# Attention scores and output rows on quarters of the TensorE array, and smaller background steps, in a fused two-layer kernel

## The chip, the cores and the metric

The kernel runs on one core of a Trainium2 chip. A core has TensorE (PE, matmul, with its weight loads shown as PEld), VectorE (DVE), ScalarE (ACT), GpSimd (POOL) and SyncE (SP), which issues transfers. They run side by side and wait for each other through semaphores. The metric is the device time of one execution in microseconds; the profile is of one such execution.

## The reference

Two layers on x of 2 x 512 x 32 x 32, all in 32-bit floats. The first is an attention with deformable keys, followed by an MLP:

```python
q = _gconv1x1(xn, qw)                         # 8 groups of 64 channels
off = tanh(pw @ gelu(depthwise 6x6, stride 4 of q)) * 4      # 8x8 key positions per group
kv = _grid_sample(xn, nx, ny)                 # 64 sampled keys per group
k = _gconv1x1(kv, kw); v = _gconv1x1(kv, vw)
bias = sign(pos) * log1p(abs(pos))            # pos: 1024 queries x 64 keys x 2, per group
bias = relu(bias @ cpb_w1 + cpb_b1)           # 128 wide
bias = relu(bias @ cpb_w2 + cpb_b2)           # 128 x 128
bias = bias @ cpb_w3 + cpb_b3
attn = softmax(qh @ kh^T * DH**-0.5 + bias)   # 16 groups (2 images x 8 heads)
x = x + out_w @ (attn @ v) + out_b
x = x + mlp(bn(x))                            # 512 -> 2048 -> 512
```

The second layer is a full self-attention over the 1024 positions of each image with 512 channels. The bias network is the largest part: for each of the 16 groups, 1024 x 64 pairs pass through a 128 x 128 layer.

## The kernel before, in words

**The loop.** 256 slices (`NS = NG * NSL`), 16 for each of the 16 groups; a slice holds four keys against all 1024 queries. In each slice VectorE makes the first layer (`st_layer1`, L616), TensorE multiplies by `cpb_w2` (`st_layer2`, L633): four PSUM tiles `ps2` of 128 x 1024, each made of two times four matmuls that use 32 columns of the array each. ScalarE empties them with a relu (L640 and L642), VectorE adds pairs (`st_sum`, L650), and transfers with addition join them further (`st_fold` L664, `st_join` L667 and L669, and L652). The pool `zp` has three PSUM tiles, shared by the slices' tiles and by all background work (`flat`); `simp` has two tiles of half that size, for the scores. Every fourth slice a table is loaded from DRAM (`load_tables`, L587, buffer `fb`, one deep) and turned into two by ScalarE (`st_tables`, L597 and L604). Every fourth slice, too, `st_layer3` adds the third layer's result of four slices into the score tile `sim` of the group (L698).

**Scores.** In the last `st_layer3` of each group four matmuls add queries times keys into `sim` (L682). The keys lie in `kz` with zeros in the half of the 128 rows that belongs to the other group, so all 128 rows of the array are used, with 32 columns a matmul.

**Background.** `later()` yields small steps, one per slice, issued behind the slice's last eviction (`tc.issue_after(evicted[s][1])`). It runs five chains (`CHAINS`), each for one or two pairs of groups. `chain` makes the queries (L265, copied by L270), the 36 taps of the depthwise convolution on ScalarE (L312; `TAPS` says how many taps go into a step, each once per pair), the offsets, and stores the logarithms for the tables to DRAM (L391, from the result of L389). `sample` weighs and samples the keys (L412 to L461), and multiplies them: keys by L468, output rows (values already multiplied by the output weights, `uo`) by L469, copied by L470 and L473. The sampled keys stand in `kvz`, zeroed by GpSimd (L451), with each group's in its own half of the columns.

**Softmax.** `softmax_steps` is a second generator, advanced once per slice: the scores leave PSUM (L712), are turned (L723, L725), then the maximum (L730, L731), exponentials (L736), reciprocals (L741), normalisation (L745), and the turning back into `qa` (L754, L757). For most pairs both groups go together (n = 2). One `tail` is active at a time.

**Start.** Ahead of the loop come the ranks (L206 to L222), which sort the 128 hidden channels by the sign of their weights for `arrange`; the first chain, step by step (`head`); and products of the second layer's weights (`weights`, L521). ScalarE's and SyncE's queues issue the input transfers in the order of the code; one that needs a semaphore already in use waits for the earlier transfer.

**After the loop** stand the output projection (L875), the MLP (L928) and the second layer (L1047, L1123, L1145).

A scheduler fixes each engine's order when the program is built; the code's order, the pools and `issue_after` decide it. The functions that the change touches, with their lines:

Of the kernel before, what the change touches and what calls it, by code (L numbers as in the profile page):

```python
# [8 lines left out]
F32 = mybir.dt.float32  # L9
# [10 lines left out]
J = 64  # L20
# [5 lines left out]
CHAINS = [[(0, 0)], [(0, 1)], [(0, 2), (0, 3)], [(1, 0), (1, 1)], [(1, 2), (1, 3)]]  # L26
HEAD = 3
TAPS = [36, 12, 6, 4, 4]
NU = 4
# [18 lines left out]
def conv_seq_kernel(ctx: ExitStack, tc: tile.TileContext, x, xt, kst, pst, cst, vec, wsm, outw, w1, w2, wl, out):  # L48
    nc = tc.nc


# [28 lines left out]

    kz = cp.tile([P, NCH * B, 2, J], F32, name="kz")

# [56 lines left out]
    with tc.tile_pool(name="lp", bufs=2) as lp:  # L139
# [27 lines left out]
        nc.scalar.dma_start(out=ws[:, 0:P], in_=wsm[:, 0:P])  # L167
        nc.scalar.dma_start(out=ws[:, 1024:1408], in_=wsm[:, 1536:1920])
        nc.scalar.dma_start(out=cs, in_=cst)

# [3 lines left out]
        )  # L174
        nc.scalar.dma_start(out=pz[:, 0:413], in_=pst)
        nc.scalar.dma_start(out=ident, in_=kst)

        def load(b, k):
# [26 lines left out]
        perm, place = pw_[:, 256:384], pw_[:, 384:512]  # L205
        nc.gpsimd.memset(one, 1.0)  # L206
        nc.gpsimd.tensor_scalar(po_, wb[:, 0:1], 0.0, None, ALU.is_ge)
        ps = flat("rank")
        nc.tensor.matmul(ps[:, 0:1], tri, po_, start=True, stop=True)
        nc.tensor.matmul(ps[:, 512:513], one, po_, start=True, stop=True)  # L210
        nc.scalar.copy(rn, ps.rearrange("p (h n) -> p h n", h=2)[:, :, 0])
        r_, n_ = rn[:, 0:1], rn[:, 1:2]
        nc.gpsimd.tensor_scalar(pc, chan, n_, r_, ALU.add, ALU.subtract)
        nc.gpsimd.tensor_scalar(dc, pc, r_, po_, ALU.subtract, ALU.mult)
        nc.gpsimd.tensor_tensor(pc, pc, dc, ALU.subtract)
        nc.vector.tensor_scalar(k16, four, n_, 4.0, ALU.is_le, ALU.mult)
        nc.vector.tensor_reduce(t4, k16, AX.X, ALU.add)
        free, bound = ([t.rearrange("p (a b l) -> p b a l", a=2, b=2)[:, i] for t in (place, crow)] for i in (0, 1))
        nc.vector.tensor_scalar(bound[0], bound[1], t4, 64.0, ALU.is_ge, ALU.mult)
        nc.vector.tensor_tensor(bound[0], bound[0], bound[1], ALU.add)  # L220
        nc.vector.tensor_scalar(free[0], free[1], t4, None, ALU.add)
        nc.vector.tensor_scalar(perm, place, pc, None, ALU.is_equal)  # L222

# [24 lines left out]
        def chain(ci):  # L248
# [3 lines left out]
            for i in range(K):  # L252
                k = k0 + i
                if i == 0:
                    xn = xn0 if ci == 0 else load(b, k)
                    yield
                nc.scalar.activation(xn, xn, AF.Identity, bias=col("bn1b", k), scale=bns[:, k : k + 1])
                if ci > 0:
                    yield
                ps = flat("psq")  # L260

                quads = [(slice(64 * f, 64 * f + 64), slice(64 * h, 64 * h + 64), f, h)
                         for f in range(2) for h in range(2)]
                for f_, h_, f, h in quads:
                    nc.tensor.matmul(  # L265
                        ps[h_, f * 512 : (f + 1) * 512], wq[f_, k * P + 64 * f : k * P + 64 * f + 64],
                        xn[f_, h * 512 : (h + 1) * 512], start=True, stop=True,
                    )
                for f_, h_, f, h in quads:
                    nc.scalar.copy(  # L270
                        qa[f_, b, k, h * 512 : (h + 1) * 512], ps[h_, f * 512 : (f + 1) * 512]
                    )
                if i + 1 < K:
                    xn = load(b, k + 1)
                yield
# [123 lines left out]
        def sample(ci):  # L399
# [23 lines left out]
            for i, (b, k) in enumerate(G):  # L423
# [20 lines left out]
                for t in range(8):  # L444
                    for f in range(2):
# [3 lines left out]
                        )  # L449
                kvz = ph.tile([P, 2, J], F32, name="kvz")  # L450
                nc.gpsimd.memset(kvz, 0.0)  # L451

                for f in range(2):
                    r = slice(64 * f, 64 * f + 64)
                    d = kvz[r, f, :].rearrange("p (e i t) -> p e i t", e=2, t=8)
                    v, u = (
# [8 lines left out]

                ps = flat("pkk")
                kf = kvz.rearrange("p f j -> p (f j)")
                nc.tensor.matmul(ps[:, 0:P], wk[:, k * P : (k + 1) * P], kf, start=True, stop=True)  # L468
                nc.tensor.matmul(ps[:, 512:1024], kf, uo[:, k, :], start=True, stop=True)  # L469
                nc.scalar.activation(  # L470
                    kz[:, g].rearrange("p f j -> p (f j)"), ps[:, 0:P], AF.Copy, scale=DH ** (-0.5)
                )
                nc.scalar.copy(vp[:, g, :], ps[:, 512:1024])  # L473
                yield
# [83 lines left out]
        head, g, n, v = chain(0), weights(0), weights(1), vectors()  # L558
        for _ in range(HEAD):
            next(head)  # L560
        next(g)
# [110 lines left out]
        def st_layer3(s):  # L672
            gi, i = divmod(s // 4, NSL // 4)
            b, k, f = groups[gi]
            if i == 0:
                sims[gi] = simp.tile([P, 512], F32, name="sim")
            if i == NSL // 4 - 1:
                assert state[chain_of[b, k][0]] is None
                for h in range(2):
                    for e in range(2):  # L680
                        q = 64 * h + 32 * e
                        nc.tensor.matmul(  # L682
                            sims[gi][q : q + 32, :], kz[:, b * NCH + k, f, 32 * e : 32 * e + 32],
                            qa[:, b, k, h * 512 : (h + 1) * 512], start=False, stop=False,
                        )
            w = w3f[:, 24 - 8 * i : 56 - 8 * i]
# [6 lines left out]
            for m in range(len(parts[1])):  # L693
                for h in range(2):
                    for e in range(2):
                        if m < len(parts[e]):
                            q, (w_, t) = 64 * h + 32 * e, parts[e][m]
                            nc.tensor.matmul(  # L698
                                sims[gi][q : q + 32, :], w_, t[:, h, :], start=(i == 0),
                                stop=(i == NSL // 4 - 1 and m == len(parts[e]) - 1),  # L700
# [5 lines left out]
        def softmax_steps(gi):  # L706
# [27 lines left out]
            for a in range(8):  # L734
                for i in range(n):
                    nc.scalar.activation(  # L736
                        e[:, a, i], e[:, a, i], AF.Exp, bias=mx[:, a, i : i + 1], accum_out=sm[:, a, i : i + 1]
                    )
                if a % 2 == 1:
                    yield  # L740
            nc.vector.reciprocal(sm[:, :, 0:n], sm[:, :, 0:n])  # L741
            yield
            for a in range(8):
                for i in range(n):
                    nc.scalar.activation(e[:, a, i], e[:, a, i], AF.Copy, scale=sm[:, a, i : i + 1])  # L745
                if a % 4 == 3:
                    yield
# [12 lines left out]

        tail = None
        bg = later()
# [4 lines left out]
        for s in range(NS):  # L767
# [31 lines left out]
            if bg is None and s > ready and (s - ready) % 4 == 0 and (s - ready) // 4 <= 8:  # L799
# [3 lines left out]
                else:  # L803
                    fold(nc.vector, op0[0], which=(i - 4,))
            if tail is not None:
                with tc.issue_after(evicted[s][s % 4 == 0]):
                    tail = tail if next(tail, 0) is None else None
            if s % 4 == 3 and s >= 7:
                st_layer3(s - 7)
                if (s - 3) % NSL == 0:  # L810
                    tail = softmax_steps(s // NSL - 1)
        st_sum(NS - 1, 2)
        st_layer3(NS - 4)
        tail = softmax_steps(NG - 1)
        next(tail)
# [515 lines left out]
```

## Time and profile before

| | |
|---|---|
| median of 3 runs | 2697.14 us (2695.79 to 2699.49) |
| profiled execution | 2695.95 us, span 2694.2 us |
| first to last tile of L633 | from 45.2 us to about 1945 us |
| passes of L633 | 16384, busy 1784.1 us |
| passes of L682 (queries times keys) | 128, busy 17.3 us |
| passes of L468 and L469 (keys, output rows) | 16 and 16, busy 3.9 and 8.2 us |
| ACT L312 / L736 / L745 | taps / exponentials / normalisations of the background |
| granted TensorE clock | 0.999 |

A row of the profile gives line, engine, operation, output<-input by the program's names, shapes, count, busy time and mean duration of one, then the engine's idle time before it and what ended it. A matmul of 32-bit floats appears as two passes, so 16384 passes are 8192 matmuls. Four matmuls on different columns or quarters of the array run together: their passes start a few ns apart. In the timeline the columns are start, length, engine and operation; SPq is SyncE's queue of transfers. The ends of matmuls are modelled.

### The profile page before, as it was taken

Reading aid. Unit: us, or ns where it says so; the run is one execution under the profiler, and the core shown is the slowest. Engines: PE = TensorE matmul, PEld = TensorE weight load, DVE = VectorE, ACT = ScalarE, POOL = GpSimd, SP = SyncE. Lnnn points to the kernel's source line nnn. Section 1 sums busy time; section 2 is a strip of 40 time slices with the busy share of each in tenths; the row PEclk is TensorE's granted clock in tenths of the full one; section 3 lists DMA queues with packets and bytes.
Section 4 is the critical chain, followed back from the end, with each engine's and each line's share of the span. In section 5 each row is a group of like instructions: output and inputs, shape, how many; then the busy total and the mean of one; then the engine's idle time right before and its main releaser. Section 6 shows DMA issues by size and latency. Waiting matters only on the chain.

```text
span 2694.2 us, 47017 instructions
## 1 busy us (share of the span) xinstructions
PE 2668.7 (99%) x19644; PEld 961.0 (36%) x19644; DVE 2239.4 (83%) x1337; ACT 1681.3 (62%) x2166; POOL 575.6 (21%) x625
## 2 busy tenths in 40 slices
PE   9999999999999999999999999999999999999999
PEld 3323323333432333233333333333344444446455
DVE  5999999998999899999999999999764484466354
ACT  4788797789878887877777786787622131114041
POOL 1222222222222222222222222222243223000000
PEclk9999999999999999999999999999999999999999
DMA  5667666766666766767677676776631110000000
GB/s 186 149 146 148 155 139 137 159 147 147 141 146 146 154 137 137 155 141 149 141 155 145 143 152 145 148 150 141 128 128 47 47 47 31 16 16 0 31 1 31
DMA packets 95219, 314.05 MB, mean 117 GB/s; under 512 B 17184, under 2 KB 19872, under 8 KB 92320
## 3 DMA queue, kind: packets, MB, share of 16 engines
q0 software_dynamic: 57168, 201.88, 40.2%
q1 hardware_dynamic: 36832, 108.02, 11.3%
q8 instruction: 155, 2.54, 0.4%
q10 hardware_dynamic: 1008, 1.15, 0.1%
q14 instruction: 56, 0.46, 0.0%
HBM read 71.67 MB, written 6.55 MB: 29 GB/s over the span
## 4 chain that ended last, share of the span: by engine, by line
PE 88%; ACT 4%; DMA 3%; issue 2%; DVE 2%; POOL 0%; ACTq 0%; DVEq 0%; POOLq 0%; SPq 0%
PE ps L633 57%; PE sw L928 14%; PE sw L1047 9%; PE sim L698 2%; PE sw L1145 2%; DMA ua<-ua 1%; DMA ua<-uo 1%; PE psg L521 1%; PE sw L875 1%; ACT prod L312 1%; ACT rx L640 1%; DVE h L616 1%; ACT ub L642 1%; PE sim L682 0%; ACT sx L745 0%
## 5 line engine op out<-in xcount | busy, mean ns | idle before, releaser
L633 PE MATMUL ps<-h,cw 128*32 128x512 f32 x16384 | 1784.1, 593 | 14.6 <-ACT rx L640 14.2
L616 DVE CUSTOM_DVE_ANT_1 h<-ta,tb 128x4096 f32<-128x4096 f32 (+1 forms) x257 | 1132.3, 4406 | 47.4 <-PE ps L633 43.1
L633 PEld LDWEIGHTS ps<-h,cw 128*32 128x32 f32 x16384 | 536.2, 110 | 1231.3 <-issue 1130.1
L640 ACT ACTIVATE rx<-ps,sc 128x1024 f32<-128x1024 f32 x512 | 568.7, 1111 | 203.2 <-PE ps L633 187.8
L642 ACT ACTIVATE ub<-ps,sc 128x1024 f32<-128x1024 f32 x256 | 307.9, 1203 | 89.8 <-PE ps L633 89.4
L650 DVE SCALAR_TENSOR_TENSOR ub<-rx,sc,ub 128x1024 f32<-128x1024 f32 x256 | 327.6, 1280 | 5.8 <-ACT ub L642 5.6
L652 POOL DMA_DIRECT2D ua<-ub x128 | 114.7, 896 | 726.9 <-DVE ub L650 698.8
L652 POOL DMA_DIRECT2D uo<-ub x127 | 117.6, 926 | 388.0 <-DVE ub L650 317.5
L928 PE MATMUL sw<-xb,w1t 128*128 128x512 f32 x448 | 193.7, 592 | 1.3 <-DVE xs L121 1.3
L928 PE MATMUL sw<-hm,w2t 128*128 128x512 f32 x448 | 193.6, 592 | 0.0
L642 ACT ACTIVATE ua<-ps,sc 128x1024 f32<-128x1024 f32 x128 | 154.0, 1203 | 57.1 <-PE ps L633 56.8
L642 ACT ACTIVATE uo<-ps,sc 128x1024 f32<-128x1024 f32 x128 | 153.9, 1202 | 40.1 <-PE ps L633 38.0
L650 DVE SCALAR_TENSOR_TENSOR ua<-rx,sc,ua 128x1024 f32<-128x1024 f32 x128 | 164.1, 1282 | 16.4 <-ACT ua L642 16.3
L669 POOL DMA_DIRECT2D ua<-uo x126 | 108.4, 861 | 321.2 <-DMA ua<-uo 306.1
L650 DVE SCALAR_TENSOR_TENSOR uo<-rx,sc,uo 128x1024 f32<-128x1024 f32 x128 | 164.1, 1282 | 11.8 <-ACT uo L642 11.7
L121 DVE TENSOR_TENSOR hm<-hm,sw 128x1024 f32<-128x1024 f32 x56 | 67.6, 1219 | 112.5 <-PE sw L928 112.3
L664 POOL DMA_DIRECT2D ua<-ua x126 | 152.7, 1212 | 5.3 <-DMA ua<-ub 4.2
L928 PEld LDWEIGHTS sw<-xb,w1t 128*128 128x128 f32 x448 | 85.0, 190 | 108.8 <-issue 104.8
L937 ACT ACTIVATE hm<-hm,vs 128x512 f32<-128x512 f32 x64 | 42.6, 713 | 129.5 <-DVE hm L121 129.5
L928 PEld LDWEIGHTS sw<-hm,w2t 128*128 128x128 f32 x448 | 85.1, 190 | 107.1 <-issue 106.2
L121 DVE TENSOR_TENSOR xs<-xs,sw 128x1024 f32<-128x1024 f32 (+1 forms) x48 | 55.5, 1171 | 74.6 <-PE sw L1047 36.0
L1047 PE MATMUL sw<-aT,vt 128*128 128x512 f32 x224 | 96.7, 593 | 0.3 <-ACT aT L1127 0.3
(238 smaller groups left out, 1797.8 us busy)
## 6 DMA issues: line engine op xcount, KB each, us to landing
ua<-ub POOLq DMA_DIRECT2D x128, 512.0 KB, 4.8
uo<-ub POOLq DMA_DIRECT2D x127, 512.0 KB, 5.0
fb<-fdr SPq DMA_DIRECT2D x64, 512.0 KB, 5.3
ua<-ua POOLq DMA_DIRECT2D x126, 256.0 KB, 6.3
ua<-uo SPq DMA_DIRECT2D x126, 256.0 KB, 2.4
ua<-uo POOLq DMA_DIRECT2D x126, 256.0 KB, 4.0
w1t<-in_w SPq DMA_DIRECT2D x8, 1024.0 KB, 4.9
w2t<-in_w SPq DMA_DIRECT2D x8, 1024.0 KB, 4.8
```

The source lines that it names most:

```text
L121: nc.vector.tensor_tensor(out, a, b_, op)
L616: nc.vector._custom_dve(TENSOR_ADD_SAT, out=h1[:, y : y + step].rearrange("p y t x -> p (y t x)"), in0=a.unsqueeze(1).to_broadcast([P, ste ...
L633: nc.tensor.matmul(ps[32 * q : 32 * q + 32, h, :], cw2[:, 32 * z : 32 * z + 32], h1[:, 16 * h : 16 * h + 16, q, :], start=True, stop=True,)
L640: nc.scalar.activation(o, ps, AF.Relu, bias=sc[:, 4 + z : 5 + z])
L642: nc.scalar.activation(o, ps, AF.Relu, bias=sc[:, 4 + z : 5 + z], scale=sc[:, z : z + 1])
L650: nc.vector.scalar_tensor_tensor(r[1], r[0], sc[:, z : z + 1], r[1], ALU.mult, ALU.add)
L652: nc.gpsimd.dma_start(out=sums[s][1], in_=sums[s][3], accum_op=ALU.add)
L664: nc.gpsimd.dma_start(out=lanes(s, 0), in_=lanes(s, 1), accum_op=ALU.add)
L669: nc.gpsimd.dma_start(out=lanes(s, 1), in_=lanes(s + 1, 0), accum_op=ALU.add)
L698: nc.tensor.matmul(sims[gi][q : q + 32, :], w_, t[:, h, :], start=(i == 0), stop=(i == NSL // 4 - 1 and m == len(parts[e]) - 1),)
L928: nc.tensor.matmul(ps[:, m, :], w[:, a, k, m * P : (m + 1) * P], x[:, b_, k, :], start=(k == 0), stop=(k == 1),)
L1047: nc.tensor.matmul(ps[:, m, :], w[:, a, k, c + m * P : c + (m + 1) * P], x[b_][:, k, :], start=(k == 0), stop=(k == nk - 1),)
```

## The change

Five edits:

1. `kz` holds each pair's keys without zeros, 64 columns. In the last `st_layer3` of the first group of a pair, four matmuls of 64 rows and 64 columns (`QUADS`) give queries times keys of both groups, and the second group's score tile is taken then.
2. In `sample` the keys stand in `kv` without zeros or memset; keys are one matmul of 64 columns, output rows four matmuls of 64 x 64 with 256 columns each, in a PSUM tile of their own, copied by four instructions.
3. `TAPS` goes from 6, 4, 4 to 4, 3, 3 for the last three chains.
4. With two groups together the softmax yields after every pair of exponentials and every fourth normalisation; waiting generators stand in the list `tails`, since one now takes more than 16 slices.
5. The ranks become `rank()`, called after the first chain's queries; two input transfers change places.

```diff
-TAPS = [36, 12, 6, 4, 4]
+TAPS = [36, 12, 4, 3, 3]
...
+    QUADS = [(slice(64 * f, 64 * f + 64), slice(64 * h, 64 * h + 64), f, h) for f in range(2) for h in range(2)]
...
-    kz = cp.tile([P, NCH * B, 2, J], F32, name="kz")
+    kz = cp.tile([P, NCH * B, J], F32, name="kz")
...
         nc.scalar.dma_start(out=ws[:, 0:P], in_=wsm[:, 0:P])
-        nc.scalar.dma_start(out=ws[:, 1024:1408], in_=wsm[:, 1536:1920])
-        nc.scalar.dma_start(out=cs, in_=cst)
...
         nc.scalar.dma_start(out=pz[:, 0:413], in_=pst)
+        nc.scalar.dma_start(out=ws[:, 1024:1408], in_=wsm[:, 1536:1920])
         nc.scalar.dma_start(out=ident, in_=kst)
+        nc.scalar.dma_start(out=cs, in_=cst)
...
+        def rank():
...
-                kvz = ph.tile([P, 2, J], F32, name="kvz")
-                nc.gpsimd.memset(kvz, 0.0)
+                kv = ph.tile([P, J], F32, name="kv")
...
-                ps = flat("pkk")
-                kf = kvz.rearrange("p f j -> p (f j)")
-                nc.tensor.matmul(ps[:, 0:P], wk[:, k * P : (k + 1) * P], kf, start=True, stop=True)
-                nc.tensor.matmul(ps[:, 512:1024], kf, uo[:, k, :], start=True, stop=True)
-                nc.scalar.activation(
-                    kz[:, g].rearrange("p f j -> p (f j)"), ps[:, 0:P], AF.Copy, scale=DH ** (-0.5)
-                )
-                nc.scalar.copy(vp[:, g, :], ps[:, 512:1024])
+                ps, pk = flat("pkv"), flat("pkk")
+                nc.tensor.matmul(pk[:, 0:J], wk[:, k * P : (k + 1) * P], kv, start=True, stop=True)
+                for f_, h_, f, h in QUADS:
+                    nc.tensor.matmul(
+                        ps[h_, f * 512 : f * 512 + 256], kv[f_, :], uo[f_, k, h * 256 : (h + 1) * 256],
+                        start=True, stop=True,
+                    )
+                nc.scalar.activation(kz[:, g], pk[:, 0:J], AF.Copy, scale=DH ** (-0.5))
+                for f_, h_, f, h in QUADS:
+                    nc.scalar.copy(vp[f_, g, h * 256 : (h + 1) * 256], ps[h_, f * 512 : f * 512 + 256])
...
-        for _ in range(HEAD):
-            next(head)
+        next(head)
+        next(head)
+        rank()
+        next(head)
...
-            if i == 0:
+            if gi not in sims:
                 sims[gi] = simp.tile([P, 512], F32, name="sim")
-            if i == NSL // 4 - 1:
+            if f == 0 and i == NSL // 4 - 1:
...
-                for h in range(2):
-                    for e in range(2):
-                        q = 64 * h + 32 * e
-                        nc.tensor.matmul(
-                            sims[gi][q : q + 32, :], kz[:, b * NCH + k, f, 32 * e : 32 * e + 32],
-                            qa[:, b, k, h * 512 : (h + 1) * 512], start=False, stop=False,
-                        )
+                sims[gi + 1] = simp.tile([P, 512], F32, name="sim")
+                for f_, h_, o, h in QUADS:
+                    nc.tensor.matmul(
+                        sims[gi + o][h_, :], kz[f_, b * NCH + k, :], qa[f_, b, k, h * 512 : (h + 1) * 512],
+                        start=(o == 1), stop=False,
+                    )
...
-                if a % 2 == 1:
+                if n == 2 or a % 2 == 1:
                     yield
...
-                if a % 4 == 3:
+                if a % (4 // n) == 4 // n - 1:
                     yield
...
-            if tail is not None:
+            if tails:
                 with tc.issue_after(evicted[s][s % 4 == 0]):
-                    tail = tail if next(tail, 0) is None else None
+                    if next(tails[0], 0) is not None:
+                        tails.pop(0)
...
-                    tail = softmax_steps(s // NSL - 1)
+                    tails.append(softmax_steps(s // NSL - 1))
```

## The prediction

> **What bounds the kernel now.** I read the busy times first, then the same by stage, then the waits of TensorE (PE), then the rows and the timeline of what the change touches.
>
> ```profile
> span 2694.2 us, 47017 instructions
> ...
> PE 2668.7 (99%) x19644; PEld 961.0 (36%) x19644; DVE 2239.4 (83%) x1337; ACT 1681.3 (62%) x2166; POOL 575.6 (21%) x625
> ...
> PE 88%; ACT 4%; DMA 3%; issue 2%; DVE 2%; POOL 0%; ACTq 0%; DVEq 0%; POOLq 0%; SPq 0%
> ```
>
> PE is busy nearly always and carries 88% of the chain that ended last. The rest of the chain shows where PE had to wait. By stage (columns: stretch, length, then busy time of PE, weight load, VectorE, ScalarE, GpSimd):
>
> ```profile
> 1000.00:1200.00 200.00, 197.62 (x1860) 61.16 (x1856) 197.45 (x115) 160.33 (x222) 47.69 (x55) 1.00 0.68 145
> 1200.00:1947.00 747.00, 747.00 (x6948) 228.73 (x6944) 706.59 (x329) 553.86 (x646) 181.43 (x206) 1.00 0.69 145
> ```
>
> From 1200 us on, when the chains are finished, PE never stops; all its idle time lies before. The main wait of PE between 45 and 1200 us (us in total, times, longest):
>
> ```profile
> PE ps L633 <- ACT rx L640: 14.2, 13, 2.7
> ```
>
> So in the loop PE waits for ScalarE (ACT) to empty PSUM, 13 times; two more waits are of 0.2 us. These gaps count only what lies beyond modelled ends. By the starts of consecutive passes (normally 0.43 us from group to group) I get 18.6 us in 17 places, a cold-clock stretch at 833 us included. ACT's timeline shows the cause at one of them:
>
> ```profile
> 151.22 1.21 ACT L642 ACTIVATE ub<-ps,sc 128x1024 f32<-128x1024 f32 x1 [0.60 <-PE ps L633]
> 152.32 3.59 ACT L312 ACTIVATE prod<-qa,vs 128x49 f32<-128x49 f32 x12
> 155.81 1.10 ACT L640 ACTIVATE rx<-ps,sc 128x1024 f32<-128x1024 f32 x1
> ```
>
> Twelve taps hold ACT 3.5 us between two evictions, and PE's next tile starts 0.82 us late (0.93 a slot later). So ACT may be away about 2.65 us before PE notices.
>
> **What the Trainium skill says.** "TensorEngine Tiling (Array Packing)", Tiling Modes, has four independent 64x64 tiles, and says that changing the tiling mode drains TensorE. The trace agrees: the L265 quads run together, and PE's steps into and out of them are longer (below). Its Performance Considerations warn that tiling doesn't speed up PSUM evacuation; the waits above are of that kind. "ScalarE: Activation LUTs", What ACT_TABLE_LOAD costs, gives 1283 ns a table load; here it takes 1.28 us.
>
> **The change, part by part.** PE first. Starts in PE's timeline and in the rows by form:
>
> ```profile
> 195.85 1.04 PE L682 MATMUL sim<-qa,kz 128*32 128x512 f32 x8
> 196.71 1.04 PE L698 MATMUL sim<-ua,w3f 128*32 128x512 f32 x8
> ...
> 604.35 1.09 PE L265 MATMUL psq<-xn,ws 64*64 64x512 f32 x8
> 605.37 3.64 PE L633 MATMUL ps<-h,cw 128*32 128x512 f32 x32
> ...
> 297.61 0.49 PE L468 MATMUL pkk<-kvz,ws 128*128 128x128 f32 x2
> 297.93 1.02 PE L469 MATMUL pkk<-vp,kvz 128*128 128x512 f32 x2
> 298.89 7.50 PE L633 MATMUL ps<-h,cw 128*32 128x512 f32 x68
> ```
>
> *Queries times keys.* Before, 16 groups of four 32-column matmuls, in the mode of their neighbours: 0.86 us each (195.85 to 196.71), 13.7 us. After, 8 groups of four 64x64 matmuls of the form of L265: 1.02 us (604.35 to 605.37), 0.11 more at the entry (0.52 from the last L633 pass to L265, against 0.41) and 0.02 behind: 1.16 us, 9.3 us. Gain 4.5 us, not the 6.9 us that halving would give; two mode changes take the rest.
>
> *Keys and output rows.* Before, 297.61 to 298.89 is 1.28 us, with entry and exit 1.42 us, 8 times. After: 64 columns instead of 128 in the first product (some 0.16 + 0.16 us, by the first steps of other small matmuls), then quads of 256 columns, half of L265's passes (0.25 us to the second pass, 0.31 us from it to L633), with one more mode change: about 1.01 us. Gain 0.4 x 8 = 3.2 us. PE's work so falls by **7.7 us**, in a stage where PE is the bound.
>
> *What this costs at PSUM.* The step now takes two of the three PSUM tiles instead of one. The next slice's first tile must then wait for the last tile of the slice before: its eviction starts 0.23 us after its end and takes 1.20 us (L642), 0.1 us to PE, so 1.5 us, while the new matmuls cover 1.0 us. 0.5 us of wait, 8 times: **+4.4 us** at 0.55 (from 0, if ACT is early, to 1.0 each where it is late). ACT itself gets four 64-partition copies of 256 (0.59 us at 512, L270; about 0.37) for one of 0.58: 0.9 us more a step, under the 2.65 us that it may be away. The memset of kvz leaves GpSimd, busy 21%: nothing.
>
> *Smaller steps.* No work is removed from ACT; pile-ups get smaller. I went through ACT's instruction order in the changed program slot by slot, with 0.29 us a 64-wide tap, 0.41 us a 128-wide, 0.33 us an exponential with its accumulator, 0.24 us a normalisation, and compared with 2.65 us:
> - chain 1 keeps its 12 taps: 1.7 us of wait stay.
> - chain 2 (slots 40 to 53): before 1.30 + 2.87 + 1.67 + 0.37 = 6.2 us. After, 8 taps with 2 exponentials or 4 normalisations, 3.3 to 3.8 us at three places, and an output transpose behind them: 0.8 + 1.1 + 0.6 + 1.1 = 3.6 us.
> - chains 3 and 4: 6 taps; 0.16 + 0.40 + 1.16 + 1.14 + 0.66 = 3.5 us become 0.6; the exponentials of slot 104 (2.69 + 1.41 us, behind a maximum that VectorE reached late) 0.7; the normalisations beside L431 and L434 (1.24 + 0.85) 0.5.
> - chain 4's gelu now falls between exponentials (slot 138), which reload their table: 2 x 1.28 us in one slot. 0.95 us become 2.4.
>
> Sum after: 1.7 + 4.4 + 3.6 + 0.6 + 0.7 + 0.5 + 2.4 = 13.9 against 18.6: **-4.7 us**.
>
> *What the finer steps make late.* Chain 2 ends three slots later, and its table is wanted in slot 60. In the trace of before:
>
> ```profile
> 473.06 0.42 DVE L389 SCALAR_TENSOR_TENSOR fe<-fe 64x256 f32<-64x256 f32 x1
> ...
> 474.62 1.41 ACT L597 ACTIVATE ta<-fb,vs 128x512 f32<-128x512 f32 x1
> ...
> 473.51 5.42 SPq L391 DMA_DIRECT2D fdr<-fe  x4
> 479.10 1.70 SPq L587 DMA_DIRECT2D fb<-fdr  x1
> ```
>
> Call E the end of L389 (473.5), in slot 56; ACT asks for a table at E + 1.1. After, the same instruction stands in slot 59, so slot 60 asks at E + 1.1 + 6.9 = E + 8. But SyncE issues four stores (to E + 5.5), then a join of two partial sums (0.5 us), then the load, which lands 5.3 us later (median of L587): E + 11.4. ACT is 3.4 us late, with the evictions of the slice behind it. Of this some 0.9 us is cover: the two table operations take 1.7 us (1.13 + 0.58 from start to start) of the 2.65 us that ACT may be away. **+2.6 us** once (0 to 6). Chains 3 and 4 end 20 slots before their tables are wanted.
>
> *Start.* PE idles at 6.9 to 9.0 us before the rank matmul, for pst (landed at 8.9); only then come the queries, whose input was ready at 7.5. The swap lets them go first, but cst now goes last (issued at about 5.4 us, landing at some 9.3 by the 3.7 us of the transfer whose place it takes), and GpSimd's hb (L188), which waits for it, stands ahead of the sign test that the ranks need: sign at 10.5, the weight products at 11.0 instead of 10.8. **+0.2 us** (-1.4 to +1.7): VectorE's convolution starts 1.9 us sooner and takes the rank's 1.4 us in, and the loop's start stays PE's (45.2).
>
> Sum: -7.7 - 4.7 + 2.6 + 0.2 = **-9.6 us**. The profiled execution took 2695.95 us, span 2694.2, the median 2697.14; the difference belongs to every run, so 2697.1 - 9.6 = **2687.5 us**.
>
> **Rivals.**
> *More:* the new waits are hidden (kv's 4.4, chain 2's 3.6, the table's 2.6, the small ones): -7.7 - 18.6 + 1.7 + 2.4 + 0.2 = -22, 2675 us. For it: PE starts later at each of them if any earlier wait has let ACT catch up. Against: the wait at kv follows from three tiles.
> *Given back:* kv waits 1.0 us each (+3.6 more) and the table 6 us (+3.4): -2.6, 2694.5 us, no difference to be told. For it: VectorE is busy 98% at 1000 to 1200 us, so late chains don't catch up.
> *Slower:* the quads don't run together. Queries times keys writes both groups' banks, the output rows read quarters of an operand. Serial, a group costs 4 x 0.86 + 0.3 = 3.7 instead of 1.16 (+2.5, 8 times: 20 us), the kv quads +1.3 x 8 = 10: 2717 us. It decides from 0.94 us more on each of the 16 groups. Against: L265 has the same rows, columns and two banks, and its eight passes start in two bunches of four, 6 ns apart.
> That the change does nothing is excluded: its program has 32 such matmuls instead of 64.
>
> **How the numbers follow.** 2687.5 has 0.62 (own range 2682 to 2692), more 0.14, given back 0.16, slower 0.08. About 0.2% (5.4 us) can be told from no change. Faster 0.76, same 0.16, slower 0.08. The range takes in "given back" and the better half of the distance to "more": 2679 to 2697.
>
> **What would show it.** Right: sim<-qa,kz with 64 passes instead of 128, about half of the busy time of L682 (17.3 us) plus mode changes; waits of PE for L640 and L642 in total some 4 to 5 us fewer, with new ones of 0.5 us at the kv steps; one wait of ACT's table (L597 before) for fb of some 3 us near 470 us; PE at 100% from 1200 us on. Wrong: passes of the new groups 0.43 us apart; no wait at the kv steps; a wait for fb over 6 us or none; the loop starting over 2 us from 45.2.

## The result, and the profile after

The changed kernel took 2690.70 us in the median (2687.49 to 2691.74), the kernel before, beside it on the same chip, 2698.18 us (2695.79 to 2699.49): a ratio of 0.9971, 95% interval 0.9954 to 0.9989, 7.5 us less (3.0 to 12.4 by the interval). The forecast was 9.6 us less. Part of that closeness is luck: 4.4 us of forecast waits did not come, while about 3 us in PE's passes and 2.1 us more for a late table came unforecast, and that table was late for another reason than the one given.

The page of the changed kernel, its first lines and its chain of work:

```profile
span 2688.9 us, 46981 instructions
...
PE 2664.8 (99%) x19628; PEld 955.2 (36%) x19628; DVE 2244.6 (83%) x1337; ACT 1689.0 (63%) x2191; POOL 575.3 (21%) x617
...
PE 85%; DVE 6%; issue 4%; ACT 2%; DMA 2%; SPq 0%; POOL 0%; DVEq 0%; POOLq 0%; ACTq 0%
```

PE is the bound as before. The same two stages (stretch, length, then busy time of PE, weight load, VectorE, ScalarE, GpSimd):

```profile
1000.00:1200.00 200.00, 196.51 (x1844) 60.41 (x1840) 199.07 (x115) 166.80 (x228) 48.09 (x54) 1.00 0.67 142
1200.00:1942.00 742.00, 742.00 (x6904) 227.79 (x6896) 703.01 (x332) 555.16 (x662) 179.71 (x204) 1.00 0.69 145
```

From 1200 us on PE never pauses, as before; all its pauses lie ahead of that. The waits of PE between 45 and 1200 us (us in total, times, longest):

```profile
PE ps L638 <- ACT rx L645: 10.7, 12, 3.0
PE ps L638 <- DVE kv L461: 1.4, 1, 1.4
```

The first is 14.2 us in 13 places in the kernel before. There are no new waits behind the steps that make keys and output rows, where eight of about 0.5 us were forecast. Their price is there, in another form. PE's timeline around one scores step and one step of keys and output rows (columns: start, length, engine, line, operation, output<-input, shape, passes):

```profile
197.49 1.09 PE L687 MATMUL sim<-qa,kz 64*64 64x512 f32 x8
198.51 1.06 PE L703 MATMUL sim<-ua,w3f 128*32 128x512 f32 x8
...
299.44 0.43 PE L468 MATMUL pkk<-kv,ws 128*128 128x64 f32 x2
299.80 0.66 PE L470 MATMUL pkv<-vp,kv 64*64 64x256 f32 x8
300.39 0.62 PE L703 MATMUL sim<-ua,w3f 128*32 128x512 f32 x1
300.84 0.62 PE L638 MATMUL ps<-h,cw 128*32 128x512 f32 x2
300.85 0.59 PE L703 MATMUL sim<-ua,w3f 128*32 128x512 f32 x1
300.85 14.32 PE L638 MATMUL ps<-h,cw 128*32 128x512 f32 x126
314.60 0.60 PE L703 MATMUL sim<-ua,w3f 128*32 128x512 f32 x3
```

The quads of queries times keys run together: 1.02 us from their first pass to the third layer. The last lines show what was not forecast. Directly behind the quads of 299.80 stands one single matmul of the third layer (L703), a quarter of a group of four; its three partners come at 314.60. Nothing fills the other three quarters of the array for 0.45 us. Six of the eight steps have such a lone quarter in the changed program's instruction list, against two groups that are split in the program before. By the rows per form of the kernel before, and then of the changed one:

```profile
L698 PE MATMUL sim<-ua,w3f 128*32 128x512 f32 x504 | 68.4, 593 | 0.0
```

```profile
L703 PE MATMUL sim<-ua,w3f 128*32 128x512 f32 x504 | 72.2, 595 | 0.0
L687 PE MATMUL sim<-qa,kz 64*64 64x512 f32 x64 | 8.7, 615 | 0.0
```

The third layer has the same 504 passes, and covers 3.8 us more time; queries times keys fell from 17.3 to 8.7 us.

To sum over the whole loop I use the starts of consecutive PE passes from the first to the last tile of the second layer (L638). Each step is put down to the operation that starts it; what goes beyond 0.43 us in a step over 0.56 us is counted as wait. So are slow groups, whose passes start about 0.81 us after those of the group before.

| us in the loop | before | after | difference |
|---|---|---|---|
| second layer (`ps`) | 1764.31 | 1766.30 | +2.0 |
| third layer (`sim<-ua`) | 55.03 | 55.77 | +0.7 |
| queries times keys | 12.90 | 8.15 | -4.75 |
| keys and output rows | 10.14 | 7.69 | -2.45 |
| waits, slow groups included | 18.61 | 16.20 | -2.4 |
| all, with what is not listed | 1898.87 | 1892.29 | -6.6 |

Of the 16 groups of queries times keys in the kernel before, the last stands behind the loop, so 12.90 us are 15 x 0.86; all 8 of the changed kernel stand in it. The longer step into a group of quads (0.52 us from the last pass of the second layer, where 0.41 is usual) counts to that last pass, so to the second layer.

The loop starts at 46.6 instead of 45.2 us, and 750.0 instead of 750.1 us lie behind it, so +1.4 - 6.6 - 0.1 = -5.3 us, the difference of the spans (2694.2 and 2688.9).

### The profile page after: what moved, and what is told of

It is laid out like the page before. It is cut to its first block, busy times and chain, and to the rows that moved or that the text cites. A ratio compares the mean times of both kernels' runs of the same rounds, so it can differ in the third digit from the quotient of the medians.

```text
span 2688.9 us, 46981 instructions
## 1 busy us (share of the span) xinstructions
PE 2664.8 (99%) x19628; PEld 955.2 (36%) x19628; DVE 2244.6 (83%) x1337; ACT 1689.0 (63%) x2191; POOL 575.3 (21%) x617
## 3 DMA queue, kind: packets, MB, share of 16 engines
q1 hardware_dynamic: 36832, 108.02, 11.2%
## 4 chain that ended last, share of the span: by engine, by line
PE 85%; DVE 6%; issue 4%; ACT 2%; DMA 2%; SPq 0%; POOL 0%; DVEq 0%; POOLq 0%; ACTq 0%
PE ps L638 54%; PE sw L937 14%; PE sw L1056 9%; DVE h L621 3%; PE sw L1154 2%; PE sim L703 2%; PE psg L524 1%; PE sw L884 1%; DVE ub L655 1%; DMA ua<-uo 1%; DVE uo L655 1%; DMA ua<-ua 0%; ACT prod L313 0%; DVE ua L655 0%; ACT rx L645 0%
## 5 line engine op out<-in xcount | busy, mean ns | idle before, releaser
L638 PE MATMUL ps<-h,cw 128*32 128x512 f32 x16384 | 1786.6, 593 | 12.3 <-ACT rx L645 10.7
L638 PEld LDWEIGHTS ps<-h,cw 128*32 128x32 f32 x16384 | 533.9, 110 | 1231.7 <-issue 1151.7
```

Source lines behind the costliest of these rows:

```text
L638: nc.tensor.matmul(ps[32 * q : 32 * q + 32, h, :], cw2[:, 32 * z : 32 * z + 32], h1[:, 16 * h : 16 * h + 16, q, :], start=True, stop=True,)
```

## The experiments

Twelve kernels, each beside the kernel before on the same chip. Its medians stood between 2697.37 and 2697.89 us in these series. "Waits" (slow groups included) and "loop" are sums as in the table above, each from one profiled execution.

| kernel | median us (range, runs) | ratio to before, 95% | waits | loop |
|---|---|---|---|---|
| before | | | 18.6 | 1898.9 |
| changed | 2690.70 (2687.49 to 2691.74, 4) | 0.9954 to 0.9989 | 16.2 | 1892.3 |
| q_only | 2694.92 (2693.33 to 2696.89, 13) | 0.9981 to 0.9998 | 21.6 | 1898.0 |
| steps_only | 2692.96 (2691.43 to 2695.78, 21) | 0.9978 to 0.9991 | 14.9 | 1893.9 |
| rank_only | 2698.96 (2694.68 to 2700.24, 13) | 0.9996 to 1.0013 | 18.9 | 1899.1 |
| no_kv | 2686.32 (2685.09 to 2687.58, 5) | 0.9946 to 0.9971 | 12.4 | 1887.9 |
| one_tile | 2686.98 (2685.31 to 2688.50, 5) | 0.9949 to 0.9976 | 14.9 | 1887.7 |
| nokv_two | 2688.91 (2686.89 to 2690.81, 5) | 0.9950 to 0.9978 | 14.5 | 1892.2 |
| taps6 | 2693.60 (2687.53 to 2695.51, 19) | 0.9977 to 0.9991 | 18.6 | 1894.9 |
| nokv_taps6 | 2690.85 (2688.54 to 2694.10, 10) | 0.9966 to 0.9985 | 17.5 | 1892.5 |
| after_split | 2691.64 (2690.56 to 2693.47, 11) | 0.9970 to 0.9987 | 15.6 | 1891.7 |
| nokv_split | 2688.39 (2686.58 to 2690.05, 5) | 0.9954 to 0.9979 | 12.0 | 1887.5 |
| one_split | 2689.08 (2687.32 to 2690.02, 6) | 0.9955 to 0.9979 | 18.8 | 1891.7 |
| after_split2 | 2691.19 (2689.82 to 2694.15, 10) | 0.9965 to 0.9984 | 18.7 | 1894.8 |

### One part alone

**q_only**: the kernel before with the quads of queries times keys alone; the keys still stand among zeros in `kz`, and the quads read their part of it.

```diff
-            if i == NSL // 4 - 1:
+            if f == 0 and i == NSL // 4 - 1:
...
+                sims[gi + 1] = simp.tile([P, 512], F32, name="sim")
+                for f_, h_, o, h in QUADS:
+                    nc.tensor.matmul(
+                        sims[gi + o][h_, :], kz[f_, b * NCH + k, o, :], qa[f_, b, k, h * 512 : (h + 1) * 512],
+                        start=(o == 1), stop=False,
+                    )
```

> The kernel before with edit 1 alone: queries times keys of both groups on quarters, read from the zero-padded keys. Theory (PE is the bound, a quarter group costs 1.16 us with its two mode changes): 16 x 0.86 = 13.7 us become 8 x 1.16 = 9.3 us, so 4.5 us less than before, and the loop's waits stay at 18.6 us. Rival (VectorE, busy 98% beside PE, takes the gain back in the loop): under 1.5 us less. Rival (halving counts alone): 6.9 us less.

2.6 us faster (0.5 to 5.1 by the interval), though the matmuls themselves gave 4.8 (12.90 to 8.10). In the profiled execution, the steps into the quads took 0.9 of that, and waits rose from 18.6 to 21.6 us: the pile-up on ScalarE near 364 us is now followed by four slow groups (1.5 us), as the one near 834 us is in both kernels; the latter is 0.5 us longer, and three small waits, 0.8 us in all, are new near 327, 1084 and 1094 us. That execution (2696.35 us) was 1.4 us above the median of its kernel, and slow groups need not come in each execution (last section). So the waits stayed neither at 18.6 us, as expected, nor is it shown that the edit always lengthens them; the expected 4.5 us lies within the interval.

**steps_only**: edits 3 and 4 alone (`TAPS`, the softmax's yields, `tails`).

```diff
-TAPS = [36, 12, 6, 4, 4]
+TAPS = [36, 12, 4, 3, 3]
...
-                if a % 2 == 1:
+                if n == 2 or a % 2 == 1:
```

> The kernel before with edits 3 and 4 alone (fewer taps a step, finer softmax). Theory (waits of PE for ACT fall, but chain 2's table comes late once, 3.2 us and a slow-clock stretch of 1.5 us behind it): 2 to 5 us less than before, one wait of ACT for fb of about 4 us. Rival (finer steps only move the waits): within 1 us of before.

4.5 us faster: waits 3.7 us fewer, and 1.8 us in the passes of the second and third layer, since this program has no split group left (the kernel before has two). So the smaller steps paid in PE's order too, not only in waits.

**rank_only**: edit 5 alone.

```diff
-        for _ in range(HEAD):
-            next(head)
+        next(head)
+        next(head)
+        rank()
+        next(head)
```

> The kernel before with edit 5 alone. Theory (the loop starts when PE is through with its weight products, and when these run at full clock differs from run to run, 45.2 to 47.2 us with and without the edit): within 1.5 us of before, the rank matmul after the queries and a wait for GpSimd of 1.5 us ahead of it. Rival (the ranks cost the 1.4 us by which the changed kernel's loop started later): 1.4 us more.

No difference. The loop of that run starts at 45.5 us. Over all runs, with the ranks moved or not, it started between 45.2 and 47.9 us; the +1.4 us of the changed kernel's profiled execution is inside that spread and is not the ranks'. The granted clock goes with it. Ahead of the loop it is 0.50 for 3.41 us in six of the fourteen traces, and there the loop starts at 45.2 to 46.4 us; in the other eight it is 0.50 for 6.83 us, and there the loop starts at 46.6 to 47.9 us. Both kinds come with the ranks moved and not moved. In the changed kernel's trace six steps of the weight products (L524) take about twice their 0.43 us, in the trace of before three: 1.2 us more.

### The keys and output rows

**no_kv**: the changed kernel with edit 2 undone (keys with zeros, one matmul of 512 columns for the output rows, one PSUM tile). **one_tile**: edit 2 kept, but both products in one PSUM tile. **nokv_two**: no_kv, with its first product put in a second PSUM tile, so the second tile without the quads. First the edit of one_tile to the changed kernel, then that of nokv_two to no_kv:

```diff
-                ps, pk = flat("pkv"), flat("pkk")
+                ps = flat("pkk")
+                pk = ps[:, 256:512]
```

```diff
-                ps = flat("pkk")
+                ps, pk = flat("pkv"), flat("pkk")
-                nc.tensor.matmul(ps[:, 0:P], wk[:, k * P : (k + 1) * P], kf, start=True, stop=True)
+                nc.tensor.matmul(pk[:, 0:P], wk[:, k * P : (k + 1) * P], kf, start=True, stop=True)
```

> The changed kernel with edit 2 undone (zero-padded keys, 128 columns and one full 512-column product, one PSUM tile). Theory (the step's shorter matmuls, 3.2 us, are paid back by single quarter matmuls of the third layer that now stand behind it, 3.8 us in the row of sim<-ua,w3f): time stays within 1 us of the changed kernel, that row's busy time falls from 72.2 to 68.4 us or less. Rival (the gain of the step is real, and the shortfall comes from the finer steps): 3.2 us more than the changed kernel.

> The changed kernel with keys and output rows of a step in one PSUM tile instead of two (keys in columns 256 to 319). Theory (the second tile is what makes the next slice wait, and the third layer's single quarter matmuls that fill the wait cost 0.9 us each): the row of sim<-ua,w3f falls from 72.2 to about 68.4 us or less, and the time by some 3.8 us against the changed kernel. Rival (the wait is for ACT's four copies, not for the tile): no difference within 1 us, and waits of PE for ACT at these steps instead.

> The changed kernel with edit 2 undone, but the first product of the step in a second PSUM tile; the matmuls are those of the run no_kv. Theory (the second tile alone splits the third layer's groups): six single quarters again, sim<-ua,w3f from 65.9 to about 72 us, and 3 to 5 us more than no_kv. Rival (the split comes from the step being shorter or from four copies): as no_kv within 1 us.

no_kv is the fastest of all, 11.2 us under before and 4.4 under the changed kernel, where within 1 us of it, or 3.2 us more, was expected; one_tile is 3.7 under the changed kernel with the very same matmuls. Putting a second tile into no_kv costs 2.6 us, a little under the 3 to 5 expected. So it is the second tile that costs, with the quads or without. PE's timeline of one_tile at the step shown above:

```profile
298.20 0.43 PE L469 MATMUL pkk<-kv,ws 128*128 128x64 f32 x2
298.56 0.66 PE L471 MATMUL pkk<-vp,kv 64*64 64x256 f32 x8
...
312.91 1.04 PE L704 MATMUL sim<-ua,w3f 128*32 128x512 f32 x8
```

and its row of the third layer:

```profile
L704 PE MATMUL sim<-ua,w3f 128*32 128x512 f32 x504 | 65.9, 595 | 0.0
```

The lone quarter is gone; the eight passes of the third layer stand together. By the sums, the second and third layer take 1765.32 + 53.53 us in one_tile against 1766.30 + 55.77: 3.2 us for six lone quarters, 0.54 us each (0.9 was expected), where a whole group takes 0.86. In another pair of runs, after_split and one_split, it is 3.3 us. nokv_two has the six split groups back (row 72.1 us), so the second tile splits them without the quads too. The price of a split is not the same there: the two layers take 1766.96 + 53.67 us against 1765.52 + 53.53 in no_kv, 1.6 us or 0.26 each, since behind the full product of 512 columns the next passes of the second layer start 0.12 us after the lone quarter, behind the quads 0.45 us. Of the 4.3 us between the loops of nokv_two and no_kv, 2.1 are waits, 1.5 of these slow groups.

The quads of edit 2 are shorter (7.66 against 10.14 us), and yet one_tile is no faster than no_kv: one_tile's waits are 2.5 us longer, 1.8 of it in one place, 2.1 us near 1149 us against 0.3. Whether the quads have a part in that place is open. steps_only has the same wait without them (2.1 us near 1155), so they are not needed for it. But among the kernels with edits 1, 3, 4 and 5 all five with the quads have it (2.1 to 2.7 us; the changed kernel, one_tile, after_split, one_split, after_split2), and none of the three without (0.3 us; no_kv, nokv_two, nokv_split). ScalarE, SyncE and GpSimd of the changed kernel there:

```profile
1151.62 0.72 ACT L413 ACTIVATE sg<-th,edge 128x512 f32<-128x512 f32 x1 [2.40 <-DMA fdr<-fe]
...
1154.15 1.92 PE L638 MATMUL ps<-h,cw 128*32 128x512 f32 x16 [1.94 <-ACT rx L645]
...
1144.76 4.18 SPq L392 DMA_DIRECT2D fdr<-fe  x4
...
1144.17 0.90 POOL L657 DMA_DIRECT2D ua<-ub  x1 [5.72 <-DVE ub L655]
```

and of no_kv:

```profile
1147.45 0.72 ACT L413 ACTIVATE sg<-th,edge 128x512 f32<-128x512 f32 x1 [0.58 <-DMA fdr<-fe]
...
1141.03 2.70 SPq L392 DMA_DIRECT2D fdr<-fe  x4
...
1141.82 0.90 POOL L656 DMA_DIRECT2D ua<-ub  x1 [5.72 <-DVE ub L654]
```

In the changed kernel GpSimd's transfer of a slice (512 KB) is issued 0.6 us ahead of the chain's stores, and they land only after it, the last 6.8 us after the first was issued. In no_kv they are issued 0.8 us ahead of it, two of the four land before it, and the last after 6.3 us. ScalarE's sampling weights wait for the last of them, with the evictions behind. A shift of a us or so in what two queues issue decides 2 us here. What sets that shift in each program I did not follow.

### Chain 2's late table

The place where the forecast put 2.6 us. ScalarE, PE, SyncE and GpSimd in the changed kernel's timeline:

```profile
503.65 1.28 ACT L602 ACTIVATE ta<-fb,vs 128x512 f32<-128x512 f32 x1 [4.06 <-DMA fb<-fdr]
...
506.47 5.77 PE L638 MATMUL ps<-h,cw 128*32 128x512 f32 x36 [3.00 <-ACT rx L645]
...
493.04 6.00 SPq L392 DMA_DIRECT2D fdr<-fe  x4
499.27 0.51 SPq L672 DMA_DIRECT2D ua<-uo  x1
499.89 5.88 SPq L592 DMA_DIRECT2D fb<-fdr  x2
...
490.72 1.20 POOL L669 DMA_DIRECT2D ua<-ua  x1
492.97 0.90 POOL L657 DMA_DIRECT2D ua<-ub  x1 [1.05 <-DVE ub L655]
```

The logarithms were ready at 493.01 (call it E), and the table landed at E + 10.6 where E + 11.4 was forecast. ScalarE waited 4.06 us for it (forecast 3.4), PE 3.2 us. The next four groups were slow, 0.81 us instead of 0.43, 1.5 us more; the granted clock was 0.50 there (last section). Two ways to take the wait away were tried.

**taps6**: the first chain of two pairs keeps its six taps a step, so its stores come three slots earlier. **nokv_taps6**: the same on no_kv.

```diff
-TAPS = [36, 12, 4, 3, 3]
+TAPS = [36, 12, 6, 3, 3]
```

> The changed kernel with chain 2 at 6 taps a step as before (TAPS 36, 12, 6, 3, 3). Theory (chain 2's table is late by its three extra slots): the wait of ACT for fb (4.1 us) and PE's wait of 3.2 us with the slow-clock stretch (1.5 us) behind it go; chain 2's pile-ups, 12 taps with 2 exponentials or 4 normalisations, come back by 1 to 2 us; 2 to 4 us less than the changed kernel. Rival (the pile-ups that come back cost as much): within 1 us.

> The changed kernel with edit 2 undone and chain 2 at 6 taps: edits 1, 4, 5 and the half of 3. Theory (gains add): no_kv (2686.3) less the 2 to 4 us of chain 2's late table: 2683 us. Rival: no better than no_kv.

Both missed their expectations: the wait for `fb` is gone, and taps6 is 2.9 us slower than the changed kernel, nokv_taps6 4.5 slower than no_kv. The steps behind all came three slots earlier and piled up elsewhere: 2.2 us near 362, 1.2 near 405, 2.6 near 853, 3.6 near 1068 us. The last one in taps6's timeline:

```profile
1065.59 1.28 ACT L741 ACT_TABLE_LOAD   x1 [4.31 <-DVE mx L736]
...
1068.38 5.89 PE L638 MATMUL ps<-h,cw 128*32 128x512 f32 x28 [3.45 <-ACT rx L645]
```

ScalarE's list holds an exponential ahead of two evictions; VectorE's maximum comes 4.3 us late, the exponential needs a table load of 1.28 us (the Trainium skill, "ScalarE: Activation LUTs", What ACT_TABLE_LOAD costs, has 1283 ns), and PE stands until the evictions are done. So this test changed more than the wait it was for, and doesn't price it.

**after_split, nokv_split, one_split**: two stores moved from SyncE to GpSimd, but of the chain with twelve taps instead of the one whose table is late.

```diff
-                nc.sync.dma_start(
+                (nc.gpsimd if ci == 1 and c >= 2 else nc.sync).dma_start(
```

> The changed kernel, with two of the four stores of the second chain's logarithms issued by GpSimd instead of SyncE; nothing moves on TensorE, ScalarE or VectorE's lists. Theory A (the late table costs TensorE 3.2 us of wait and 1.5 us of slow groups behind it): the load is issued some 2.5 to 3 us sooner, ScalarE waits 1.0 to 1.6 us for fb instead of 4.1, TensorE's wait near 506 us and the slow groups behind it go: 4 to 4.7 us faster than the changed kernel, about 2686. Theory B (as with six taps, another pile-up takes the place of the wait that goes): within 1.5 us of the changed kernel, about 2690, with a new wait later in the list.

> The changed kernel with the keys and output rows as before, and the same two stores on GpSimd's queue. There TensorE waits 2.6 us for the late table, with no slow groups behind. Theory A: 2.6 us less than without the split stores, 2683.7. Theory B: no difference, 2686.

> The changed kernel with keys and output rows of a step in one PSUM tile, and the same two stores on GpSimd's queue. TensorE waits 3.2 us for the late table there. Theory A: 3.2 to 3.5 us less than without the split stores, 2683.6, as fast as the version with keys and output rows as before. Theory B: no difference, 2687.

That chain's table isn't late, so they say nothing of the late one. They do show how far a median moves with another series, another chip and an edit that the late table has nothing to do with: +0.9, +2.1 and +2.1 us against the kernels they were made from. Differences of two us between series are therefore not told from nothing here. Among themselves, in one series on one chip, nokv_split and one_split are 3.3 and 2.6 us under after_split; together with 4.4 and 3.7 in the other series, the second tile's cost stands.

**after_split2**: the same for the right chain.

```diff
-                nc.sync.dma_start(
+                (nc.gpsimd if ci == 2 and c >= 2 else nc.sync).dma_start(
```

> The three runs before this moved the stores of the chain with twelve taps by mistake (its table is not late), so they tested nothing of the late table; they show what such an edit does by itself. This one moves two of the four stores of the first chain of two pairs, whose table is late, from SyncE's queue to GpSimd's. TensorE's, ScalarE's and VectorE's lists are unchanged. Theory A: the load is issued some 3 us sooner, ScalarE waits about 1 us for fb instead of 4.1, TensorE's wait of 3.2 us near 506 us goes and no slow groups follow it; no other wait changes by over 0.5 us: waits in the loop 16.2 to about 12 us, the time 3 to 4.7 us under the changed kernel's. Theory B: another wait takes its place, as with six taps: waits stay at 15 to 17 us.

Neither theory holds. TensorE's, ScalarE's and VectorE's lists are the same as the changed kernel's; SyncE is free sooner and issues the load sooner, but the wait stays. SyncE, GpSimd and ScalarE in its timeline:

```profile
492.37 2.08 SPq L392 DMA_DIRECT2D fdr<-fe  x2
496.81 0.51 SPq L672 DMA_DIRECT2D ua<-uo  x1
497.49 7.87 SPq L592 DMA_DIRECT2D fb<-fdr  x2
...
492.88 1.64 POOL L392 DMA_DIRECT2D fdr<-fe  x2
...
503.24 1.28 ACT L602 ACTIVATE ta<-fb,vs 128x512 f32<-128x512 f32 x1 [4.27 <-DMA fb<-fdr]
```

E is 492.34 here. The load goes out at E + 5.2 instead of E + 6.9 and lands at E + 10.9 instead of E + 10.6. It is not SyncE's issuing that makes the table late. The DMA engines in the changed kernel (stretch, length, the five engines' busy time, PE's clock, then DMA share and GB/s):

```profile
492.00:494.00 2.00, 2.00 (x24) 0.65 (x20) 2.00 (x3) 1.11 (x1) 0.90 (x1) 1.00 1.09 203
494.00:496.00 2.00, 2.00 (x26) 0.53 (x18) 2.00 (x1) 1.21 (x1) 0.00 (x0) 1.00 0.93 155
496.00:498.00 2.00, 2.00 (x24) 0.64 (x20) 2.00 (x2) 1.12 (x1) 0.00 (x0) 1.00 1.09 186
```

From 492 to 498 us they are full, with three transfers of a slice (two of 512 KB, one of 256 KB) issued by GpSimd between 490.1 and 493.0. The stores, 64 KB in all, landed between 497.7 and 500.7 in the changed kernel and between 496.8 and 500.3 in after_split2, whichever queue issued them, and the load 2.9 us after the last of them both times. That the transfers of the slice hold them up fits both traces; moving those transfers was not tried.

## Why the prediction was right or wrong

- *Queries times keys*: right. A group takes 1.02 us and 0.11 more at the entry (0.52 us from the last L638 pass, against 0.41), 1.13 for the forecast 1.16: 16 x 0.86 less 8 x 1.13 is 4.7 us (forecast 4.5).
- *Keys and output rows*: mechanism right, too large by 0.75 us: 2.45 instead of 3.2. From the first pass to the next work a step takes 0.96 us for 1.27 before, each with 0.11 at the entry. The mis-sized terms are the first product with 64 columns, 0.37 us instead of 0.32, and the quads behind it, 0.59 instead of 0.56.
- *What this costs at PSUM*: the step that failed. The forecast put the second tile's price into eight waits for evictions of 0.5 us. No such wait appeared; "no wait at the kv steps" was among the prediction's own signs of being wrong. The price (about 3.2 us of PE's time in the trace; 3.7 us in the median of one_tile, 2.6 in that of one_split) is in the order of the program instead: with two tiles the scheduler sets a single quarter of the third layer behind six of the eight steps, and behind quads such a quarter costs more than half of a group. The prediction had priced each instruction in the company that it had before, and had not read PE's list behind the step. That a second tile causes the split is shown by one_tile and nokv_two; why the scheduler then picks one quarter is not.
- *Smaller steps*: forecast 13.9 us of waits without the late table, 4.4 of them at the steps above, so 9.5 elsewhere; measured 16.2 less 4.7 for the late table, 11.5. Twelve taps: 1.7 forecast, 1.76 measured (0.83 and 0.93 us near 158 and 166). Chain 2: 3.6 forecast, 2.3 measured. Chain 4's gelu with its tables: 2.4 forecast, 1.1 measured. Not seen at all: 1.6 us near 876 us (the wait put down to `kv`), and 2.1 us near 1154, where the steps' later place meets the stores' landing. The total of all waits with the table is near (2.1 us fewer forecast, 2.4 measured) because the 4.4 us that did not come and what the others cost more cancel; that is luck.
- *Chain 2's late table*: that it comes, its lateness (E + 10.6 for E + 11.4) and ScalarE's wait (4.06 for 3.4 us) were right; PE lost 3.2 us and 1.5 in slow groups instead of 2.6. The reason was wrong: the working counted SyncE's four issues, a join and a load in a row, and after_split2 cut 1.7 us from that row without moving the landing. Why the sum agreed all the same is only argued: the issue times in it came from a stretch of the trace of before (473.5 to 479 us) in which the DMA engines were as full (share 1.01 to 1.09 from 472 to 480 us), so they may have held that wait already. The place was named wrongly as well, near 470 us: three slots later it is near 500.
- *Start*: no effect of the ranks, as forecast within its bounds; the 1.4 us by which the loop starts later go with the longer stretch at half clock (rank_only), which the forecast did not have. The queries came at 7.56 us and the weight products at 11.04 (11.0 forecast):

```profile
7.56 1.09 PE L266 MATMUL psq<-xn,ws 64*64 64x512 f32 x8 [1.04 <-ACT xn L260]
...
10.17 0.59 PE L212 MATMUL rank<-pwork,pz 128*128 128x1 f32 x2 [1.53 <-POOL pwork L210]
11.04 13.12 PE L524 MATMUL psg<-wl_s 128*128 128x512 f32 x24
```

- *The rivals*: the quads do run together, so "slower" is out. "More" asked for the new waits to be hidden; no_kv and one_tile, at -11.2 and -10.5 us, show how much of it was there once the second tile is left out, though not by hidden waits: 12.4 and 14.9 us of waits remain. "Given back" had the right suspect, the step of keys and output rows, with the wrong mechanism.

By its sum the prediction had -7.7 for PE's matmuls, -4.7 for waits, +2.6 for the table and +0.2 for the start. The trace has -7.2, then +3.0 for passes of the second and third layer and the offsets' small matmuls (entries into quads, lone quarters), -2.4 for all waits with the table, +1.4 for the start and -0.1 behind the loop.

## What to carry to other kernels

When an edit takes one more tile from a pool that other work shares, read the bound engine's instruction list behind it, not only its waits: here the scheduler filled the gap with part of a group that only pays whole. Edits that shorten PE's work and edits that split the work it covers may need each other: no_kv, which has both, gave 11.2 us, q_only and steps_only 2.6 and 4.5, though the intervals leave open whether that is more than their sum. Before moving a transfer to another queue, look whether the DMA engines have room in that stretch: here, where they were full, an earlier issue landed no earlier. And before a wait in one trace is put down to an edit, look at the granted clock behind it and at where that execution stands among the others.

## What the runs showed of the hardware that was not expected

- The slow groups of the second layer, 0.81 to 0.84 us apart instead of 0.43, stand where the granted clock is 0.50 (1.00 is full speed). The columns are as before, PE's clock third from the end; first the changed kernel, then the kernel before:

```profile
508.00:510.00 2.00, 2.00 (x15) 0.45 (x9) 2.00 (x2) 1.97 (x4) 0.00 (x0) 0.50 0.98 156
834.00:836.00 2.00, 2.00 (x16) 0.58 (x12) 1.97 (x3) 0.93 (x1) 0.00 (x0) 0.50 1.03 197
```

What decides it can be read from the fourteen traces, though no run was made to test it. A stretch at 0.50 in the loop lasts 3.41 us or twice that, and within a run such stretches start a whole number of 3.41 us apart (in the changed kernel at 9.41 and 507.76 us, 146 times). Cut the loop into pieces on that grid: each of the 13 pieces at clock 1.00 in which PE idled 61 to 96% is followed by a piece at 0.50, and none of the 15 with 40 to 59% is (idle time by the modelled ends). So the place of a pause on the grid counts, not only its length: 3.4 us in one_tile, spread 35% and 59% over two pieces, had no slow groups behind it; 2.4 us in one_split, 64% of one piece, had four. The grid stands elsewhere in each trace (the first stretch at 0.50 starts at 8.6 to 12.3 us), so 1.5 us of slow groups may come in one execution of a kernel and not in another.

- One matmul on 32 columns whose three partners run elsewhere costs 0.54 us on average behind the quads (the changed kernel against one_tile) and 0.26 behind a full product of 512 columns (nokv_two against no_kv), against 0.86 us for the four together.
- The first two stores of the late table, of 16 KB each, took 4.7 and 6.6 us from issue to landing with the DMA engines full (492 to 498 us), and one of the same kind 2.0 us where it was issued just ahead of the slice's transfer (no_kv, 1141.03 to 1143.06).
